# Forming block products for pairs of groups in a four-layer graph kernel

## The chip, the cores and the metric

The kernel runs on one NeuronCore of a Trainium2 chip. The metric is device time in microseconds of one execution, and lower is better. TensorE (PE in the profile) multiplies matrices into PSUM; VectorE (DVE), ScalarE (ACT) and GpSimd (POOL) do elementwise work; SyncE (SP) issues the DMAs. PSUM is used as eight banks of 512 fp32 values on each of 128 partitions. Everything is fp32.

## The reference

The input is a batch of 128 graphs of 64 nodes with 512 features, and a dense 64x64 adjacency for each graph. Four layers follow each other. Each adds its output to its input and then applies a layer norm over the features.

```python
# layer 0: graph attention with additive scores
y = x @ w;  s = y @ a
A = tanh((s_i + s_j) / 8) * 8;  A = leaky(A);  A = exp(A) * adj
A = A / sum(A) * sum(adj);      out = A @ x @ w
# layer 1: attention with adjacency as a factor
weight = adj * exp(q @ k.T);    out = (weight / sum(weight)) @ v
# layer 2: agg = adj @ (k * mask);  w = scale * mask * sum(q * agg)
out = softmax(w) * v
# layer 3: two hypergraph convolutions, 512 -> 1024 -> 512
h = layer_norm(relu(D H B H.T (x @ W1.T) + b1))
out = D H B H.T (h @ W2.T) + b2 + x
# after each layer
x = layer_norm(x + out)
```

The kernel rewrites these. In layers 1 and 2, q @ k.T becomes x @ (Wq.T Wk) @ x.T, so that one 512x512 matrix (m1, m2) is made once and stands for two. The graph operators, which are 64x64, are applied ahead of the dense products.

## The kernel before

**Tiling.** The 8192 rows (128 graphs of 64 nodes) form 64 tiles of 128 rows. Two tiles are a *group* (`GT = 2`, 256 tokens), so there are `NG = 32` groups. Two groups are a *pair* (`SG = 2`), and two groups share a chunk of adjacency (`GC = 2`).

**Seven products for eight.** A dense product of a group is cut into 2x2 blocks, and done with seven block products in place of eight, by sums of the left blocks (`side_sums`, L915) and sums of the weights' blocks (t1 to t4, made once by `combine`, L527). `seven_products` (L953) calls `products_of` (L957), whose inner `times` (L967) emits the matmuls of one block product. It holds two banks, which go on accumulating from product to product: after each one its bank is evicted by `first` (the first write to a block of the result) or `more` (an addition to it), and only then may the next product add to that bank. A third bank takes the one product that stands apart.

**Row blocks before.** In a single group the two row blocks are its two tiles, 128 tokens each. A block product has 128 tokens, 256 features in depth (512 for 3b) and 256 output columns, so half a bank is filled. For w0, v1, v2 and 3b a block of tokens is the stationary operand and 256 columns of weights move past it (`width = D // 2`, L963). For m1 and m2 (`across=True`) the result is wanted transposed: blocks of weights are stationary, and the 128 tokens move:

```python
for c in range(2):
    for k in range(chunks):
        nc.tensor.matmul(o[:, ts(c, P)], b[:, k, ts(c, P)], l[:, k, :], ...)
```

Evictions go through `scaled_into` (L1019, w0, v2, 3b: one scaled add on DVE of 128x256), `plain_into` (L1032, v1) and `z_into` (L1199, m1, m2: ACT writes, DVE adds).

**Steps of a group.** `run(g)` (L1226) goes from step 0 to 12: scores of layer 0 (0), gathering x by the graph (1, `gathered` L893), w0 and layer norm (2), transposes (3), m1 and v1 (4), scores (5), attention and layer norm (6), transposes (7), m2 (8), scores (9), softmax (10), v2 and layer norm (11), gathering for layer 3 (12). Each step works on one group. After two groups, `run_rest(n)` (L1354) does layer 3 for both: 3a by two levels of the seven-product scheme, 49 small products with the two groups as row blocks (`pair_left_side` L941, `forty_nine_products` L1104), then bias, relu and layer norm of each h (13), gathering (14) and 3b (15). 3b loads each weight piece once for the pair but multiplies each group apart. The pairs in `APART_3A`, which hold groups 0, 1, 30 and 31, do layer 3 with groups alone.

**Weights.** m1 and m2 stay in SBUF (`RESIDENT`). The pieces of w0, v1, v2, 3a and 3b lie in DRAM and are loaded by `streamed` (L748) into the tiles called ring when a product needs them; w0, v1 and v2 are three loads of 512 KB and one of 256 KB for each group.

**Order.** Operations are not emitted in the order of the code. `order.add` records each with its engine, an estimated cost and a key (`BASE[g]` + step - `EARLY[step]`). `Order.run` then plans all five engines: it goes forward in planned time and starts on each free engine the ready operation with the lowest key, if there are free tiles for it. The kinds of tiles and their number (L334 to L344: x 6, k4 17, ring 9, bank 8, ...) set how much may be under way, and at most three products at once are (`kinds["product"]`, L345). The plan also knows the array's division: most matmuls use all 128x128 of it, gathers use 64x64 quarters, scores use 64-column halves, and a change between them has a planned price. `pinned` (L1473) then fixes the order of each engine. All traced lines are therefore that helper's, L1479, and operations are told apart by tiles and shapes. `PREPARED` and `LEAD` shift the preparation of weights and the halves of a pair's layer 3.

Of the kernel before, what the change touches and what calls it, by code (L numbers as in the profile page):

```python
# [13 lines left out]
ALU = mybir.AluOpType  # L14
# [17 lines left out]
    3.2735, 8.0652, 5.7526, 12.3539, 15.2711, 19.4819, 28.2783, 26.7823,  # L32
    36.0674, 38.5696, 41.9228, 44.5673, 49.736, 57.2555, 62.3073, 66.8928,
    72.8672, 74.4107, 83.6469, 85.3215, 91.7972, 98.2815, 105.3829, 104.8263,
    113.3204, 117.0908, 123.649, 125.591, 132.4907, 135.1692, 144.8875, 142.169,
# [3 lines left out]
LEAD = [18.6707, 10.0037]  # L39
PREPARED = [3.2501, 6.4884, 8.4096, 18.9837, 15.9208, -1.3348]  # L40
# [29 lines left out]
class Order:  # L70
    LATENCY = {"PE": 210, "DVE": 125, "ACT": 140, "POOL": 120, "SP": 3500}
    AGAIN = {"PE": 0, "DVE": 115, "ACT": 115, "POOL": 120}
    TO_PE = 0
    BYTES_PER_NS = 270
    UNDERWAY = 9
    TURN, TURN_DIVIDED = 110, 60

    NEAR = 0.004
    FAR = 163.3543
    ENOUGH = 1.2457  # L80

    EARLY = [7.5201, -0.713, 2.7673, 21.1569, 0.5055, 0.6085, 5.6889, 14.9021, 0.0162, 18.6753, 16.5455, 0.4227, -1.4983, -1.1338, 12.9793, -2.8031]
# [3 lines left out]
    AHEAD = 5.2259  # L86
    TOGETHER = 0.3719
    OLDEST = 3.3813
    SPARE = {"k4": 1, "ring": 0}
# [35 lines left out]
    def keys_by_what_follows(self):  # L125
# [15 lines left out]
        for o in self.ops:  # L141
            if o.led and o.group is not None:
                gone = self.TOGETHER * (o.step - o.led.step)
                o.step, o.key = o.step - gone, o.key - gone

# [150 lines left out]
def kernel(  # L296
# [37 lines left out]
    kind("x", 6, GT, D)  # L334
    kind("k4", 17, PIECE)
    kind("ring", 9, PIECE)
# [430 lines left out]


# [457 lines left out]
    def run(g):  # L1226

        def step(k):
            order.key, order.early, order.group = BASE[g] + float(k), order.EARLY[k], g

        step(0)
        xt = xs.pop(g)
        adj, turned, gm, am, sums, g1, dc, dh = prepared[g // GC]
        own = slice(g % GC * GT, g % GC * GT + GT)
        at_x = block_views(xt, lambda: xt.t)
        of_x = lambda t: xt[[2 * t, 2 * t + 1]], lambda t, rows, at: xt.t[rows, t, at : at + N]


        s = Buf("col", GT)
        diag, e, ps_s = Buf("e", GT), Buf("e", GT), Buf("bank")  # L1240
        for t in range(GT):
            row_dot([xt[[2 * t, 2 * t + 1]], u0_b], s[t], lambda t=t: xt.t[:, t, :], lambda: u0_b.t)
            act(N + 40, [s[t]], [diag[t]], lambda t=t: nc.scalar.activation(diag.t[:, t], eye, AF.Identity, scale=s.t[:, t : t + 1]))

        over_graph(diag, ps_s)
        for t in range(GT):
            act(N + 40, [ps_s, s[t]], [e[t]], lambda t=t: nc.scalar.activation(
                e.t[:, t], tiles(ps_s)[:, t], AF.Tanh, bias=s.t[:, t : t + 1]), NOW)
        dve(GT * N, [e], [e], lambda: nc.vector.scalar_tensor_tensor(e.t, e.t, 0.1, e.t, ALU.mult, ALU.max))
        act(GT * N, [e], [e], lambda: nc.scalar.activation(e.t, e.t, AF.Exp, scale=8.0))  # L1250
        dve(GT * N, [e, adj], [e], lambda: nc.vector.tensor_mul(e.t, e.t, adj.t[:, own]))

        ps_e = Buf("bank")
        over_graph(e, ps_e)
        rs = Buf("e")
        dve(7 * GT * N, [ps_e], [rs], lambda: nc.vector.reciprocal(flat(rs.t), ps_e.t[:, : GT * N]), NOW)
        dve(GT * N, [e, rs], [e], lambda: nc.vector.tensor_mul(e.t, e.t, rs.t))
        step(1)
        left = left_side(gathered(*of_x, lambda h, t: e.t[halves[h][0], t, :], [e]))
        step(2)  # L1260
        sx = Buf("col", 2 * GT)
        seven_products(*left, first_use["w0"] if g == 0 else streamed("w0"), *scaled_into(
            at_x, sums, slice(2 * CT + own.start, 2 * CT + own.stop), D // 2, sx))
        layer_norm(xt, sx)


        step(3)
        xT = transposed(xt, turn=True)

        for t in range(GT):  # L1270
            pool(D, [xt[[2 * t, 2 * t + 1]], bv_b], [xt[[2 * t, 2 * t + 1]]],
                 lambda t=t: nc.gpsimd.tensor_add(xt.t[:, t, :], xt.t[:, t, :], bv_b.t))
        left = left_side(xT)
        step(4)
        zT = Buf("k4", 4)
        seven_products(*left, first_use["m1"] if g == 0 or "m1" in RESIDENT else streamed("m1"), *z_into(zT, u1_c), across=True)
        v = Buf("k4", 4)
        seven_products(*left, first_use["v1"] if g == 0 else streamed("v1"), *plain_into(v))
        step(5)
        ps_w = scores(xT, zT)  # L1280
        e1 = Buf("e")
        act(GT * N, [ps_w], [e1], lambda: nc.scalar.activation(e1.t, tiles(ps_w), AF.Exp), NOW)
        dve(GT * N, [e1, turned], [e1], lambda: nc.vector.tensor_mul(e1.t, e1.t, turned.t[:, own]))
        step(6)
        f = Buf("col")
        ps_f = Buf("bank")
        pe(110, [e1], [ps_f], lambda: nc.tensor.matmul(ps_f.t[:, :GT], flat(e1.t), row_of, start=True, stop=True))
        dve(GT, [ps_f], [f], lambda: nc.vector.reciprocal(f.t[:, :GT], ps_f.t[:, :GT]), NOW)
        po = [Buf("bank") for _ in range(GT)]
        sx = Buf("col", GT)  # L1290

        def emit_po():

            for h, (cols, _) in enumerate(halves):
                for t, (rows, _) in enumerate(halves):
                    nc.tensor.matmul(po[t].t[cols], e1.t[rows, h, :], v.t[rows, ts(h, D)], start=True, stop=True)

        pe(w_pe(D), [e1, v], po, emit_po, mode="quarters", matmuls=4)
        for t in range(GT):
            dve(D + 110, [po[t], f, xt[[2 * t, 2 * t + 1]]], [xt[[2 * t, 2 * t + 1]], sx[t]],  # L1300
                lambda t=t, sx=sx: nc.vector.scalar_tensor_tensor(
                    xt.t[:, t, :], po[t].t, f.t[:, t : t + 1], xt.t[:, t, :], ALU.mult, ALU.add, accum_out=sx.t[:, t : t + 1]), NOW)
        layer_norm(xt, sx, 1)

        step(7)
        xT2 = transposed(xt)
        left = left_side(xT2)
        step(8)
        zT2 = Buf("k4", 4)
        seven_products(*left, m2 if "m2" in RESIDENT else streamed("m2"), *z_into(zT2), across=True)  # L1310
        step(9)
        ps_w2 = scores(xT2, zT2)
        pr = Buf("e")
        dve(GT * N, [ps_w2, am], [pr], lambda: nc.vector.tensor_mul(pr.t, tiles(ps_w2), am.t[:, own]), NOW)
        step(10)

        ps_p = Buf("bank")
        over_graph(pr, ps_p)
        mx, sw, wc = Buf("col"), Buf("col"), Buf("col")
        dve(GT * N, [ps_p], [mx], lambda: nc.vector.tensor_reduce(mx.t[:, :GT], tiles(ps_p), AX.X, ALU.max), NOW)  # L1320
        dve(GT, [mx], [mx], lambda: nc.vector.tensor_scalar(mx.t[:, :GT], mx.t[:, :GT], -SCALE, None, ALU.mult), NOW)
        e2 = Buf("e", GT)
# [227 lines left out]
```

## Time and profile before

| | |
|---|---|
| median of 3 runs | 2146.41 us (2145.26 to 2149.38) |
| the profiled execution | 2145.31 us, of which the span 2143.4 us |
| instructions in the trace | 53774, of which 21433 matmul passes |
| TensorE clock granted | 0.998 of full speed |
| busy: PE 99%, weight loads 85%, DVE 66%, ACT 56%, POOL 21% | of the span |
| DMA | 418.92 MB on the main queue, 56.8% of 16 engines' span |
| loads of w0, v1, v2 | 93 + 189 of 512 KB, 31 + 63 of 256 KB |
| k,m passes (m1, m2) | 3584 of 128x128 |
| ring,k passes of 256 columns | 4828; ring,h (3b) 1024 |

A matmul row has a start and a length, but the lengths of neighbours overlap, so the time from one start to the next tells what a matmul costs in a run of its kind. PEld is the load of the stationary operand. An fp32 matmul of the code stands as two rows (passes) in the trace, a transpose as one. Names like `bank<-ring,k` say what is written and read: weights in ring against tokens in k4; `k,m` is m1 or m2, and `ring,h` is 3b or the sums that 3b lays into h.

### The profile page before, as it was taken

The numbers are of one execution on the slowest core, as the hardware profiler recorded it, in microseconds if no ns is written. First come the engines' busy times: TensorE is split into PE (matmuls) and PEld (weight loads), VectorE is DVE, ScalarE is ACT, GpSimd is POOL, SyncE is SP. The second block draws the span as 40 slices with busy tenths as digits, with TensorE's granted clock in tenths as the row PEclk, the third lists the DMA queues.
The fourth block names the chain that finished last, engine by engine and source line by source line (L and its number), as shares of the span: only waits on it lengthen the run. The fifth ranks groups of instructions, "written<-read, shape, count | busy, mean of one in ns | idle before, by whom it ended". The sixth has DMA issues, their size and how long they took to land.

```text
span 2143.4 us, 53774 instructions
## 1 busy us (share of the span) xinstructions
PE 2123.4 (99%) x21433; PEld 1829.4 (85%) x21433; DVE 1407.9 (66%) x4150; ACT 1197.9 (56%) x2698; POOL 458.0 (21%) x434
## 2 busy tenths in 40 slices
PE   8999999999999999999999999999999999999997
PEld 4887788888889888888888888888888988888875
DVE  5766667675864767667586766766777576676744
ACT  3545566473655565656455655646656456564635
POOL 1211142212211221220212202122130222203111
PEclk9999999999999999999999999999999999999999
DMA  9778866645644647456455646554554554645555
GB/s 295 229 269 303 281 226 250 208 165 183 227 163 147 205 153 244 144 191 211 156 179 183 213 145 207 181 190 165 185 200 154 199 194 152 214 164 172 179 180 179
DMA packets 166315, 422.35 MB, mean 197 GB/s; under 512 B 34929, under 2 KB 52529, under 8 KB 166065
## 3 DMA queue, kind: packets, MB, share of 16 engines
q1 hardware_dynamic: 166064, 418.92, 56.8%
q8 instruction: 169, 2.77, 0.5%
q14 instruction: 82, 0.66, 0.1%
HBM read 382.77 MB, written 36.08 MB: 195 GB/s over the span
## 4 chain that ended last, share of the span: by engine, by line
PE 99%; ACT 0%; DMA 0%; DVE 0%; issue 0%; SPq 0%; POOLq 0%; ACTq 0%; DVEq 0%
PE bank L1479 99%; DMA k<-in_wk_dram 0%; ACT k L1479 0%; SPq L1479 0%; DVE e L1479 0%; ACT h L1479 0%; ACT x L1479 0%; DVE h L1479 0%; DVE col L1479 0%; POOLq L1546 0%; ACTq L1546 0%; DVE m L1479 0%; ACT e L1479 0%; DVE x L1479 0%; ACT kept L1479 0%
## 5 line engine op out<-in xcount | busy, mean ns | idle before, releaser
L1479 PE MATMUL bank<-ring,k 128*128 128x256 f32 (+1 forms) x4940 | 1187.8, 387 | 1.3 <-ACT k L1479 1.3
L1479 PEld LDWEIGHTS bank<-ring,k 128*128 128x128 f32 x4940 | 898.2, 190 | 150.2 <-issue 28.4
L1479 ACT COPY k<-bank 128x256 f32<-128x256 f32 (+1 forms) x934 | 429.3, 485 | 402.5 <-PE bank L1479 386.3
L1479 DVE SCALAR_TENSOR_TENSOR x<-bank,col,x 128x256 f32<-128x256 f32 (+1 forms) x736 | 363.3, 504 | 281.3 <-PE bank L1479 275.2
L1479 PEld LDWEIGHTS bank<-k,m 128*128 128x128 f32 x3584 | 436.2, 192 | 19.1 <-issue 4.0
L1479 PE MATMUL bank<-k,m 128*128 128x128 f32 x3584 | 448.5, 276 | 0.0
L1479 DVE TENSOR_TENSOR k<-bank,k 128x256 f32<-128x256 f32 x582 | 236.0, 420 | 181.9 <-PE bank L1479 118.4
L1479 POOL TENSOR_TENSOR col<-col,mhalf 128x2 f32<-128x2 f32 (+1 forms) x161 | 111.9, 695 | 1139.1 <-DVE col L1479 860.8
L1479 ACT ACTIVATE k<-x,col 128x512 f32<-128x512 f32 x256 | 184.3, 722 | 253.4 <-DVE col L1479 241.7
L1479 ACT ACTIVATE x<-x,col,col 128x512 f32<-128x512 f32 x256 | 199.5, 815 | 63.3 <-DVE col L1479 63.0
L1479 PE MATMUL bank<-ring,h 128*128 128x256 f32 x1024 | 233.3, 380 | 0.0
L1479 PEld LDWEIGHTS bank<-ring,h 128*128 128x128 f32 x1024 | 192.3, 190 | 26.9 <-ACT k L1479 0.8
L1479 DVE TENSOR_TENSOR k<-k,k 128x256 f32<-128x256 f32 (+2 forms) x361 | 179.1, 505 | 0.4
L1479 DVE TENSOR_TENSOR k<-k 128x256 f32<-128x256 f32 (+2 forms) x349 | 152.9, 457 | 37.0 <-ACT k L1479 33.8
L1479 ACT ACTIVATE k<-bank,u_c 128x128 f32<-128x128 f32 x256 | 85.8, 371 | 65.7 <-PE bank L1479 60.9
L1479 PE MATMUL bank<-k,k 128*64 128x64 f32 (+1 forms) x2112 | 111.7, 239 | 4.7 <-DMA k<-in_wk_dram 4.6
L1479 POOL TENSOR_TENSOR k<-k,b3b_b 128x512 f32<-128x512 f32 x64 | 81.2, 1272 | 150.7 <-DVE k L1479 93.0
L1479 PEld LDWEIGHTS bank<-k,k 128*64 128x64 f32 (+1 forms) x2112 | 79.7, 140 | 37.3 <-issue 18.1
L1479 POOL TENSOR_TENSOR x<-x,bv_b 128x512 f32<-128x512 f32 x64 | 81.4, 1280 | 115.1 <-PE bank L1479 38.9
L1479 DVE TENSOR_SCALAR col<-col 128x2 f32<-128x2 f32 (+2 forms) x402 | 71.5, 185 | 41.2 <-ACT k L1479 34.7
L1479 DVE TENSOR_TENSOR h<-k,k 128x1024 f32<-128x1024 f32 (+1 forms) x88 | 91.0, 1041 | 7.7 <-ACT k L1479 7.2
L1479 POOL TENSOR_TENSOR x<-x,k 128x512 f32<-128x512 f32 x64 | 81.4, 1273 | 40.8 <-DVE k L1479 28.4
(102 smaller groups left out, 1627.3 us busy)
## 6 DMA issues: line engine op xcount, KB each, us to landing
ring<-3a SPq DMA_DIRECT2D x196, 512.0 KB, 4.3
ring<-v SPq DMA_DIRECT2D x189, 512.0 KB, 4.2
ring<-3b SPq DMA_DIRECT2D x126, 512.0 KB, 4.3
ring<-w SPq DMA_DIRECT2D x93, 512.0 KB, 4.4
x<-in_x_dram SPq DMA_DIRECT2D x32, 512.0 KB, 5.2
ring<-v SPq DMA_DIRECT2D x63, 256.0 KB, 4.1
out_dram<-x SPq DMA_DIRECT2D x31, 512.0 KB, 4.5
ring<-w SPq DMA_DIRECT2D x31, 256.0 KB, 4.4
```

The source lines that it names most:

```text
L1479: made = f(*args, **kwargs)
```

## The change

`run` now takes a list of groups and does all steps, 0 to 15, for them together; `run_rest` and its waiting list are gone. The groups of `APART_3A` are still run one by one, through the old functions. For the other 14 pairs each dense product is made once per pair: the two groups are the two row blocks (256 tokens each), so a block product has 256 tokens and 256 output columns and fills a bank of 512. The weights of w0, v1 and v2 are streamed once for a pair, as those of 3b were. For m1 and m2 256 tokens move past each weight block. A block product is recorded as two PE operations, one for each half of the bank.

```diff
-    kind("x", 6, GT, D)
+    kind("x", 7, GT, D)
     kind("k4", 17, PIECE)
-    kind("ring", 9, PIECE)
+    kind("ring", 8, PIECE)
...
+    def pair_products(a, s, pieces, first, more, across=False, chunks=KC // 2):
+        going, pair = Buf("product"), [Buf("bank") for _ in range(2)]
+        pieces = iter(pieces)
+        def times(token, left, start=True):
+            piece, view = next(pieces)
+            def emit(u):
+                l, b, o = left[1](), view(), token.t
+                for k in range(chunks):
+                    w, v = (b[:, k, ts(u, P)], l[:, k, :]) if across else (l[:, k, ts(u, P)], b[:, k, :])
+                    nc.tensor.matmul(o[:, ts(u, D // 2)], w, v, start=start and k == 0 and u == 0,
+                                     stop=k == chunks - 1, skip_group_check=True)
+            for u in range(2):
+                pe(w_pe(D // 2, chunks), [left[0], piece, going], [token], lambda u=u: emit(u), matmuls=chunks)
+            return (token, going), lambda: token.t
+        first("11", *times(pair[0], a["11"]))
+        first("22", *times(pair[1], s[0]))
+        more("11", *times(Buf("bank"), a["12"]))
+        first("12", *times(pair[0], s[1], False))
+        more("12", *times(pair[1], s[3], False))
+        more("22", *times(pair[0], s[2], False))
+        first("21", *times(pair[0], a["22"], False))
+
+    def pair_scaled_into(xs_, fs, sums):
+        def add(k, token, ps, last):
+            xt, (f, at), r, j = xs_[row(k)], fs[row(k)], row(k), col(k)
+            for t in range(GT):
+                cell, c = xt[2 * t + j], 2 * t + j
+                dve(D // 2 + 40 + 70 * last, [*token, f, cell], [cell, *([sums[r][c]] if last else [])],
+                    lambda t=t, c=c: nc.vector.scalar_tensor_tensor(
+                        xt.t[:, t, ts(j, D // 2)], ps()[:, ts(t, D // 2)], f.t[:, at + t : at + t + 1], xt.t[:, t, ts(j, D // 2)],
+                        ALU.mult, ALU.add, **({"accum_out": sums[r].t[:, c : c + 1]} if last else {})), NOW)
...
+    def pair_z_into(zs, bias=None):
...
+        def first(k, token, ps):
+            if bias is None:
+                act(D, [*token], [at(k)[0]], lambda: nc.scalar.copy(at(k)[1](), two(ps)), NOW)
...
+        def more(k, token, ps):
+            dve(D, [*token, at(k)[0]], [at(k)[0]], lambda: nc.vector.tensor_add(at(k)[1](), two(ps), at(k)[1]()), NOW)
...
-    def run(g):
+    def run(groups):
+        n, last_of = len(groups), groups[-1]
...
+        def left_of(xT):
+            return pair_left_side(xT) if n == SG else left_side(xT[0])
...
+        left = left_of(xT)
         step(4)
+        zT = [Buf("k4", 4) for _ in groups]
...
+        if n == SG:
+            pair_products(*left, m1_pieces, *pair_z_into(zT, u1_c), across=True)
+        else:
+            seven_products(*left, m1_pieces, *z_into(zT[0], u1_c), across=True)
+        vs = [Buf("k4", 4) for _ in groups]
+        if n == SG:
+            pair_products(*left, of_pair("v1", last_of), *pair_plain_into(vs))
...
-        products_of(sides, streamed("3b"))
...
+            pair_products(a, s_, streamed("3b"), *pair_scaled_into([xt_[g] for g in groups], scales, [sx[g] for g in groups]), chunks=KH // 2)
...
-        run(g)
-        if len(waiting) == SG or g // SG in APART_3A:
-            run_rest(len(waiting))
+        if g // SG in APART_3A:
+            run([g])
+        elif g % SG == SG - 1:
+            run(list(range(g - SG + 1, g + 1)))
```

Two smaller edits come with it. In layer 2's softmax the row sum of e2 is made by ACT with the exponential (`accum_out`), where DVE made it with a reduction. And the constants of the plan have new values:

```diff
-    3.2735, 8.0652, 5.7526, 12.3539, 15.2711, 19.4819, 28.2783, 26.7823,
+    6.0035, 8.2772, 13.2033, 17.6332, 26.0202, 27.1146, 41.4888, 43.61,
...
-LEAD = [18.6707, 10.0037]
-PREPARED = [3.2501, 6.4884, 8.4096, 18.9837, 15.9208, -1.3348]
+LEAD = [37.2697, 5.5754]
+PREPARED = [28.6382, 16.68, 12.9121, 14.55, 17.8769, 0.587]
...
-    TO_PE = 0
-    BYTES_PER_NS = 270
-    UNDERWAY = 9
+    TO_PE = 50
+    BYTES_PER_NS = 260
+    UNDERWAY = 8
...
-    NEAR = 0.004
-    FAR = 163.3543
-    ENOUGH = 1.2457
+    NEAR = 27.7595
+    FAR = 251.4563
+    ENOUGH = 0.0205
...
-    AHEAD = 5.2259
-    TOGETHER = 0.3719
-    OLDEST = 3.3813
-    SPARE = {"k4": 1, "ring": 0}
+    AHEAD = 15.591
+    TOGETHER = 0.0013
+    OLDEST = 1000000000.0
+    SPARE = {"k4": 0, "ring": 1}
```

The step constants `EARLY` and the rest of `BASE` change likewise. `NEAR`, `FAR` and `ENOUGH` govern when the planner turns from the whole array to a divided one, `UNDERWAY` how many loads may be in flight, and `SPARE` how many free tiles operations far ahead of the oldest must leave.

## The prediction

> **What bounds the kernel now.** I began with the page's busy shares and its chain of the work that ended last.
>
> ```profile
> PE 2123.4 (99%) x21433; PEld 1829.4 (85%) x21433; DVE 1407.9 (66%) x4150; ACT 1197.9 (56%) x2698; POOL 458.0 (21%) x434
> ...
> PE 99%; ACT 0%; DMA 0%; DVE 0%; issue 0%; SPq 0%; POOLq 0%; ACTq 0%; DVEq 0%
> ```
>
> TensorE's matmuls (PE) cover 99% of the span, and the chain never leaves them. But is that engine full, or only never empty? The Trainium skill ("Perfetto Trace Analysis", section "Identifying the Most-Contended Engine") warns that matmul busy time is a poor measure, because matmuls overlap, and asks for the busy share of weight loads. By that rule 85% leaves 15%, some 314 us, in which PE would wait; looser waits would then be worth more than fewer columns. So I looked at start times, which overlap cannot flatter: the timeline of PE's matmuls (start, length, engine, line, operation, tiles, shape, count).
>
> ```profile
> 643.37 3.62 PE L1479 MATMUL bank<-ring,h 128*128 128x256 f32 x16
> 646.82 3.62 PE L1479 MATMUL bank<-ring,k 128*128 128x256 f32 x16
> 650.27 3.73 PE L1479 MATMUL bank<-k,m 128*128 128x128 f32 x32
> 653.85 1.03 PE L1479 MATMUL bank<-ring,k 128*128 128x256 f32 x4
> ...
> 704.77 1.03 PE L1479 MATMUL bank<-ring,k 128*128 128x256 f32 x4
> 705.73 1.15 PE L1479 MATMUL bank<-k,k 128*64 128x64 f32 x32
> 706.81 1.99 PE L1479 MATMUL bank<-ring,k 128*128 128x256 f32 x8
> ```
>
> Sixteen 256-column passes take 646.82 - 643.37 = 3.45 us, 0.216 each; 32 passes of 128 columns take 653.85 - 650.27 = 3.58 us, 0.112 each. (The page has two such records, or passes, for each fp32 matmul in the code.) Such pitches hold throughout: I priced every pass of the program at the start-to-start time of its shape, and every change of the array's division at 0.10 us, and the sum is about 2090 us of a span of 2143. The rest is 4 us before the first matmul, some 10 in the start-up, 9.5 after the last matmul, and small pauses of 0.02 to 0.1 us spread evenly. So the row decides against the rule's reading: PE is full. The waits confirm it: these are all of PE's.
>
> ```profile
> PE bank L1479 <- DMA k<-in_wk_dram: 4.6, 2, 4.3
> PE bank L1479 <- DVE e L1479: 2.9, 2, 1.6
> PE bank L1479 <- ACT k L1479: 1.3, 1, 1.3
> PE bank L1479 <- issue: 0.6, 1, 0.6
> PE bank L1479 <- ACT x L1479: 0.4, 1, 0.4
> PE bank L1479 <- ACT m L1479: 0.3, 1, 0.3
> PE bank L1479 <- ACT kept L1479: 0.2, 1, 0.2
> ```
>
> Ten microseconds in all (columns: total, times, longest), nearly all at the very start. What shortens PE's list shortens the kernel; what relieves DVE, ACT, POOL or DMA does not, as long as no new wait appears.
>
> **The change, part by part.** Groups 0, 1, 30 and 31 still run alone; the other 28 become 14 pairs.
>
> *m1 and m2.* Each product of a single group issues 28 matmuls of 128 columns; a pair issues 28 of 256 for both groups. For 28 groups, two products and two passes, 3136 passes at 0.112 us (351.2 us) become 1568 at 0.216 (338.7): **-12.5 us**. A rule promises far more. The Trainium skill ("TensorE: Matmul & The Clock Gate", section "Back-to-back issue gap") gives, for a stream in which every matmul has its own weight load, about 81 ns at 128 columns and 131 at 512. A straight line gives 98 at 256 (my estimate from that page), so merging two saves 64 of 162, 40%, here 139 us. The trace says that weight loads are hidden already, for 0.112 is within 4% of half of 0.216. I take the row. The exact form, 256 columns of k against weights out of m, is not in the trace; the nearest row, ring,h, also has a new weight load for each pass and runs at 0.216. The ends are -12.5 and, should these run only as fast as now, 0.
>
> *w0, v1, v2, 3b.* Each piece of weights is 256 columns that move past 128 tokens, before and after; two token blocks of two groups become four blocks in one product. Passes and columns are the same: 0 us. The order of PE's instructions agrees: 2414 + 512 matmuls of 256 columns against ring tiles in both programs, 784 new ones against m, 224 of 128 columns left over for the four single groups.
>
> *Switches of the array.* Scores and gathers divide the array; each change costs PE. In the rows above the four passes before 705.73 need 0.86, so the divided ones begin 0.10 late, and these 32, which follow each other at 30 ns on average, hand back 0.11 late. The new planned order has 370 changes where the old one has 427, since longer products mean fewer seams and the constants of the plan are new: 57 x 0.10 = **-5.7 us**. The ends are 0 and -7.
>
> *Small pauses.* The trace has about 170 of 0.10 us between 256-column passes with no wait behind them, about one to 64 matmuls. With 783 fewer matmuls of 10973, some 12 go: **-1 us**.
>
> *Evictions.* These are what could hurt.
>
> ```profile
> L1479 DVE SCALAR_TENSOR_TENSOR x<-bank,col,x 128x256 f32<-128x256 f32 x672 | 318.1, 481 | 265.1 <-PE bank L1479 259.2 <-ACT k L1479 0.4
> L1479 ACT COPY k<-bank 128x512 f32<-128x512 f32 x482 | 269.3, 588 | 156.2 <-PE bank L1479 152.4 <-ACT h L1479 0.8 <-DVE k L1479 0.5
> L1479 DVE TENSOR_TENSOR k<-bank,k 128x256 f32<-128x256 f32 x582 | 236.0, 420 | 181.9 <-PE bank L1479 118.4 <-ACT k L1479 57.3 <-ACT kept L1479 0.3
> ```
>
> A full bank takes ACT 0.59 us instead of about 0.37, DVE about 0.69 (its 512-wide add out of a bank, h<-bank,h, mean 687 ns) instead of 0.42, and for w0, v2 and 3b two instructions of 0.48. PE may go on with that bank only afterwards. In the old order a waiting matmul often has just 0.86 us of other matmuls since the last one that the awaited engine needed, and PE does not stall, so the hand-overs both ways cost at most 0.86 - 0.48 = 0.38. The new need is then 0.97 for ACT, 1.07 for DVE and 1.34 for the two scaled adds. In the new order, of the 112 places where a pair's m1 or m2 goes on in a bank that must first be emptied, the shortest cover is 1.09 us and all but two have 1.3; for the sites behind a 256-wide scaled add 95% have 1.55 or more; for 3b the least is 1.73. Over all of PE's waits, those with under 0.8 us of such cover fall from 18 to 6. I cost the evictions at 0; if every one of the 84 pair products (14 pairs, six stages) lost 0.1 us, at +8.
>
> *Busy totals elsewhere.* DVE drops 126 adds out of banks net (about -19 us), turns 336 side sums of 256 into 168 of 512 (336 x 0.465 - 168 x 0.70, -39 us) and loses 32 reductions of e2 (-9), whose sums ACT now makes with 64 accumulator reads (64 x 0.19 = +12, inside ACT's idle 44%). All of it lies beside PE: 0 us.
>
> *DMA.* w0, v1 and v2 come once per pair: 42 streams fewer, each three loads of 512 KB and one of 256, together 77 of 419 MB. The queues were 57% busy and PE waited for no load after the start: 0. One ring tile fewer (8 for 9) takes cover away, but the shortest distance in matmul time from a freed ring to its first user is 5.8 us against 6.1, and a load lands in 4.3. SP also issues 168 fewer loads.
>
> *Start and tail.* The first 40 us in the new order have two matmuls directly behind an engine that needs the matmul before, where the old one has four, worth 1.7, 1.4, 0.5 and 0.3 us: **-1 us**, ends -3 and +2. The last 40 us have the same sequence of one group's 3a and 3b.
>
> **Sum:** -12.5 - 5.7 - 1 - 1 = -20.2 us, plus 1 for single short waits I cannot place: -19. The profiled execution took 2145.3 us (2 of them outside its span), which gives 2126; the median of the runs shown is 1.1 above it, so 2126 to 2127. I say 2126.
>
> **The rivals.**
> - *As summed*, 2120 to 2132: 0.73.
> - *Part is handed back* through evictions twice as long, at 0.1 to 0.2 us per pair product: 84 x 0.13 = 11 us, 2137. For it: full banks, and two scaled adds in a row. Against: the covers above. 0.12.
> - *Lockstep starves PE*, the case on the other side. Two groups now finish w0 together and both need their layer norm (two scaled adds 0.96, four small DVE steps 0.75, two squares 1.44, POOL's power 0.70, a scale of 0.82: 4.7 us and hand-overs) before m1 can begin, where before the other group's products filled in. With 14 pairs and four such places there are 56 stops. It takes 24.7/56 = 0.44 us each to be slower than before by 0.2%; at 1 us each the time is 2182. For it: 17 k4 tiles now hold pairs. The skill's "Consistent bubbles" (same page, "Identifying Performance Opportunities") says that a repeated gap can mean too few buffers. Against: seven x tiles, so a third pair is under way, and the covers listed. 0.12, of which 0.05 ends within 0.2%.
> - *Weight loads were worth more than the pitch shows*: towards the rule's -139 us, anything under 2118. 0.03.
>
> That the change doesn't do what it says is excluded by the order of instructions.
>
> **How the numbers follow.** A measurement of this kernel tells 0.2% (4.3 us) from no change. Faster: 0.73 + 0.12 + 0.03 = 0.88; same 0.05; slower 0.07. The range takes in the first case and most of the second: 2118 to 2140.
>
> **What would show it.** Right: k,m rows of 128x256 at a pitch of 0.216; PE still 99%; waits of PE within 10 us; some 77 MB less moved; busy times of DVE and ACT some 70 and 35 us lower. Wrong: waits of PE on ACT k, DVE x or DVE k that repeat in each pair, or gaps of PE at the layer norms.

## The result and the profile after

| | before | after |
|---|---|---|
| median | 2146.99 us (2145.26 to 2149.38, 4 runs) | 2114.22 us (2114.03 to 2114.51, 4 runs) |
| the profiled execution, its span | 2145.3, 2143.4 us | 2114.4, 2112.6 us |
| PE's passes | 21433 | 19867 |
| changes of the array's division, in the program | 427 | 370 |

The ratio is 0.9847, 95% interval 0.983 to 0.9864: 32.8 us faster by the medians, 30.8 by the spans of the two profiled executions. The prediction said 2126, with 2118 as the lower end, so the direction was right and the gain was more than half as large again as its sum.

The page of after, the lines that answer to those of before (busy shares; the chain that ended last; the DMA queue that moves data: packets, MB, share):

```profile
PE 2097.3 (99%) x19867; PEld 1773.1 (84%) x19867; DVE 1361.7 (64%) x3768; ACT 1168.2 (55%) x2538; POOL 458.3 (22%) x434
...
q1 hardware_dynamic: 141872, 341.83, 47.4%
...
PE 98%; ACT 1%; DMA 0%; DVE 0%; issue 0%; SPq 0%; POOL 0%; POOLq 0%; ACTq 0%; DVEq 0%
```

All of PE's waits in after (us in total, times, longest):

```profile
PE bank L1602 <- DMA k<-in_wk_dram: 5.5, 2, 4.2
PE bank L1602 <- DVE e L1602: 1.6, 2, 1.1
PE bank L1602 <- ACT k L1602: 1.0, 2, 0.7
PE bank L1602 <- ACT e L1602: 0.4, 1, 0.4
PE bank L1602 <- ACT x L1602: 0.2, 1, 0.2
```

The same engine bounds the kernel as before, with 8.7 us of waits. The loads fell from 418.92 to 341.83 MB, DVE's busy time by 46 us, ACT's by 30, and none of that shows in the chain. Seven groups of waits became five. The only one behind a layer norm's last step (ACT x, a gather that waits for its x) is 0.2 us. The new form of m1 and m2 can be read off PE's timeline (start, length, operation, shape, count):

```profile
584.30 7.07 PE L1602 MATMUL bank<-k,m 128*128 128x256 f32 x32
591.21 1.03 PE L1602 MATMUL bank<-ring,k 128*128 128x256 f32 x4
```

Thirty-two passes take 591.21 - 584.30 = 6.91 us, 0.216 each, the pitch taken from the ring rows of before.

**Where the time came from.** I gave every pass of both traces the time to the start of the next pass, took off the pitch of its shape, and sorted the rest by where it lies:

| part of PE's span (us) | before | after | difference | predicted |
|---|---|---|---|---|
| passes of m1, m2 at their pitch | 401.5 | 389.0 | -12.5 | -12.5 |
| other passes of the whole array at their pitch | 1420.0 | 1419.8 | -0.2 | 0 |
| edges of divided stretches: in, out, and from one divided form to the other (0.09 to 0.11 each) | 43.0 | 37.2 | -5.7 | -5.7 |
| divided passes, stalls among them included | 233.6 | 227.0 | -6.7 | part of "start" |
| pauses in the whole array after the first 60 us | 26.5 | 22.2 | -4.3 | -1 |
| the first 60 us, first matmul and jitter | 8.9 | 10.4 | +1.5 | -1 |
| start of the last matmul to the end of the span | 9.8 | 7.1 | -2.8 | 0 |
| sum | 2143.4 | 2112.6 | -30.8 | -20.2, +1 for unplaced waits |

The two large terms came out to a tenth of a microsecond. Both rows are counts times a pitch or an edge read in the traces, so this says that the counts and those prices were right, not that they were the whole price. Three small rows did not come out: the pauses, the divided passes and the tail.

Two things in these traces lie across the rows. Of the 57 changes that went, 36 are between the whole array and a divided one (184 divided stretches became 166) and 21 between the two divided forms, 64x64 quarters and 64-column halves (61 became 40). And the clock was not the same throughout. Two stretches of before (busy time and count of PE, PEld, DVE, ACT and POOL; then the granted clock of PE, the DMA share and GB/s):

```profile
20.00:24.60 4.60, 2.65 (x33) 1.05 (x34) 4.00 (x10) 2.54 (x12) 1.26 (x1) 1.00 0.97 359
24.70:28.10 3.40, 3.40 (x49) 2.09 (x40) 3.40 (x9) 1.42 (x3) 0.00 (x0) 0.50 0.91 234
```

For 3.4 us of its start-up before was granted half the clock, which can have cost it 1.7 us at most; after has no such stretch. This part of the gain is in the rows of the first 60 us and of the divided passes.

### The profile page after: what moved, and what is told of

Its sections match the earlier page's. It is cut to its first block, busy times and chain, and to the rows that moved or that the text cites. A ratio compares the mean times of both kernels' runs of the same rounds, so it can differ in the third digit from the quotient of the medians.

```text
span 2112.6 us, 49594 instructions
## 1 busy us (share of the span) xinstructions
PE 2097.3 (99%) x19867; PEld 1773.1 (84%) x19867; DVE 1361.7 (64%) x3768; ACT 1168.2 (55%) x2538; POOL 458.3 (22%) x434
## 3 DMA queue, kind: packets, MB, share of 16 engines
q1 hardware_dynamic: 141872, 341.83, 47.4%
## 4 chain that ended last, share of the span: by engine, by line
PE 98%; ACT 1%; DMA 0%; DVE 0%; issue 0%; SPq 0%; POOL 0%; POOLq 0%; ACTq 0%; DVEq 0%
PE bank L1602 98%; ACT k L1602 1%; DMA k<-in_wk_dram 0%; DVE e L1602 0%; ACT x L1602 0%; SPq L1602 0%; ACT e L1602 0%; ACT m L1602 0%; DVE col L1602 0%; DVE k L1602 0%; POOL col L1602 0%; DVE m L1602 0%; POOLq L1669 0%; DVE x L1602 0%; ACT bw_b L1602 0%
## 5 line engine op out<-in xcount | busy, mean ns | idle before, releaser
L1602 PEld LDWEIGHTS bank<-ring,k 128*128 128x128 f32 x4940 | 916.8, 190 | 146.8 <-issue 24.5
L1602 ACT COPY k<-bank 128x512 f32<-128x512 f32 (+1 forms) x822 | 406.7, 529 | 368.0 <-PE bank L1602 365.0
L1602 DVE SCALAR_TENSOR_TENSOR x<-bank,col,x 128x256 f32<-128x256 f32 (+1 forms) x736 | 341.3, 503 | 218.6 <-PE bank L1602 204.8
L1602 PE MATMUL bank<-k,m 128*128 128x256 f32 (+1 forms) x2016 | 426.7, 358 | 0.7 <-ACT k L1602 0.7
L1602 PEld LDWEIGHTS bank<-k,m 128*128 128x128 f32 x2016 | 347.4, 190 | 43.9 <-issue 1.9
L1602 DVE TENSOR_TENSOR k<-bank,k 128x256 f32<-128x256 f32 (+1 forms) x456 | 216.2, 494 | 158.4 <-PE bank L1602 107.4
L1602 DVE TENSOR_TENSOR k<-k,k 128x512 f32<-128x512 f32 (+3 forms) x319 | 191.6, 617 | 4.0 <-ACT k L1602 3.7
L1602 DVE TENSOR_TENSOR k<-k 128x256 f32<-128x256 f32 (+2 forms) x223 | 113.9, 526 | 61.7 <-ACT k L1602 53.5
L1602 POOL TENSOR_TENSOR k<-k,k 128x1024 f32<-128x1024 f32 (+1 forms) x31 | 72.1, 2326 | 182.0 <-DVE h L1602 65.9
L1602 ACT ACTIVATE k<-bank,u_c 128x256 f32<-128x256 f32 (+1 forms) x144 | 59.9, 445 | 65.2 <-PE bank L1602 65.1
```

The source lines that it names most:

```text
L1602: made = f(*args, **kwargs)
```

## Experiments

Eleven kernels ran. The kernel before, timed beside each batch, had medians of 2145.07, 2146.2 and 2144.88 us.

| kernel | median us (lowest to highest) | ratio to before, 95% |
|---|---|---|
| narrow_m | 2124.93 (2124.61 to 2127.41) | 0.9908, 0.9891 to 0.9924 |
| old_traffic | 2118.66 (2117.54 to 2119.16) | 0.9874, 0.986 to 0.9889 |
| before_split_tail | 2143.18 (2141.79 to 2145.76) | 0.9991, 0.9984 to 0.9998 |
| pairs_old_plan | 2231.03 (2230.21 to 2234.94) | 1.0402, 1.0387 to 1.0418 |
| more_switches | 2129.72 (2127.66 to 2129.79) | 0.9921, 0.9907 to 0.9934 |
| old_early | 2311.52 (2310.55 to 2314.24) | 1.0773, 1.0758 to 1.0788 |
| double_evict | 2138.98 (2138.56 to 2139.57) | 0.9967, 0.9955 to 0.9979 |
| no_single | 2138.45 (2137.52 to 2142.16) | 0.9967, 0.9954 to 0.9979 |
| forced_switches | 2250.95 (2250.59 to 2251.67) | 1.0495, 1.0478 to 1.0513 |
| forced_whole | 2169.83 (2169.59 to 2170.59) | 1.0117, 1.0102 to 1.0132 |
| long_blocks | 2118.69 (2117.36 to 2119.78) | 0.9877, 0.9863 to 0.9892 |

### narrow_m: is it the wider pass, and do pauses go with the number of matmuls?

The kernel after, with each matmul of a pair's m1 and m2 cut into two of 128 columns, in the same plan.

```diff
-                for k in range(chunks):
-                    w, v = (b[:, k, ts(u, P)], l[:, k, :]) if across else ...
+                for c in range(2 if across else 1):
+                    n = D // 4 if across else D // 2
+                    for k in range(chunks):
+                        w, v = (b[:, k, ts(u, P)], l[:, k, ts(c, n)]) if across else ...
```

> The changed kernel with the pairs' m1 and m2 issued as two matmuls of 128 columns each in place of one of 256; plan and order as in the changed kernel. Column theory: 1568 passes of 256 columns become 3136 of 128, so 1568 x (2 x 0.112 - 0.216) = +12.5 us, 2127. Theory that the small pauses go with the number of matmuls: besides, pauses of PE rise from 22 towards 26.5 us (the 784 matmuls are back), +4 to +5, 2131. Theory that they go with traffic or with the plan: pauses stay near 22, 2127.

Its row of m1 and m2 has the old form and count again:

```profile
L1605 PE MATMUL bank<-k,m 128*128 128x128 f32 x3584 | 438.0, 276 | 0.7 <-ACT k L1605 0.7
```

The time at pitch rises by 12.55 us (389.0 to 401.5) and the span by 10.4, to 2123.0. So the 256-column form is worth about what the pitch said. But 784 more matmuls bring no more pauses: after 60 us there are 21.5 us of them where after has 22.2. The step "one pause to 64 matmuls" is refuted.

### old_traffic: were the loads worth anything?

The kernel after, which after each piece of w0, v1 or v2 also copies that piece from DRAM to a DRAM buffer that nothing reads.

```diff
+            nc.sync.dma_start(out=idle[turns[0] % 8][:, : n * width], in_=src.t[:, : n * width])
```

> The changed kernel with a second, unused transfer of each piece of w0, v1 and v2 from DRAM to DRAM right behind the real one (208 transfers, some 95 MB); the output is unchanged and the PE order too. Theory that the pauses go with DMA traffic: pauses back at 26 us or more, 2118 to 2121. Theories of matmul count and of plan: pauses near 22, 2114 to 2115.

The queue moves 95 MB more and is busier than in before; the lines of its page and of PE's waits that changed most:

```profile
q1 hardware_dynamic: 154352, 437.27, 58.3%
```

```profile
PE bank L1610 <- ACT e L1610: 1.8, 3, 1.0
...
PE bank L1610 <- DVE x L1610: 1.1, 2, 0.8
...
PE bank L1610 <- ACT x L1610: 0.8, 1, 0.8
```

The span grows by 4.3 us, as six or so short waits on other engines; the pauses inside matmuls stay (19.9 us against 19.4). These 95 MB do not slow PE's passes. The kernel adds 208 issues and another kind of transfer, so its 4.3 us is only a rough mark for what the 77 MB saved can have been worth; the account of after leaves little room for it.

### before_split_tail: the tail

The kernel before splits the last layer norm by tiles only for `g == NG - 1`, which is group 31. This kernel does it for groups 30 and 31.

```diff
-            for among in (range(t, t + 1) for t in range(GT)) if g == NG - 1 else (range(GT),):
+            for among in (range(t, t + 1) for t in range(GT)) if g >= NG - 2 else (range(GT),):
```

> The kernel before, with the final layer norm of groups 30 and 31 both by single tiles (before: 31 alone). If the shorter tail of the changed kernel comes only from which of the two groups ends last: last matmul start to end of span falls from 9.8 to 7.1 us, the time by 2.8 us, 2144. If it comes from something else, the tail stays near 9.8 and the time at 2147.

The ends of the two timelines tell why. In before, both tiles go together (128x2, two tiles in one row of ACT):

```profile
2136.80 0.70 POOL L1479 TENSOR_TENSOR col<-col,mhalf 128x2 f32<-128x2 f32 x1 [10.30 <-DVE col L1479]
2137.53 0.16 DVE L1479 TENSOR_TENSOR col<-col,col 128x2 f32<-128x2 f32 x1 [0.88 <-POOL col L1479]
2137.72 1.52 ACT L1479 ACTIVATE x<-x,col,col 128x512 f32<-128x512 f32 x2 [1.27 <-DVE col L1479]
```

In after, the first tile is finished while the second still waits for POOL:

```profile
2107.67 0.80 ACT L1602 ACTIVATE x<-x,col,col 128x512 f32<-128x512 f32 x1
2107.80 0.15 DVE L1602 TENSOR_SCALAR col<-col 128x1 f32<-128x1 f32 x1 [0.24 <-ACT k L1602]
2108.09 0.56 POOL L1602 TENSOR_TENSOR col<-col,mhalf 128x1 f32<-128x1 f32 x1 [0.73 <-DVE col L1602]
```

So in before the planned order let group 30 end last, unsplit; in after it is group 31. Splitting both in before shortens the part behind the last matmul from 9.84 to 7.04 us, to after's 7.06. The median falls by only 1.9 us, with an interval that just excludes no change. The span of the profiled execution is 0.8 us shorter: 2.0 of the 2.8 us come back elsewhere in that trace (1.2 in the divided stretches, 0.7 in the first 60 us), and why was not looked into.

### pairs_old_plan and old_early: is lockstep a danger at all?

The code of after, with all constants of its plan set back to before's (pairs_old_plan), or only `EARLY` and `LEAD` (old_early).

```diff
-LEAD = [37.2697, 5.5754]
+LEAD = [18.6707, 10.0037]
...
-    EARLY = [14.4537, -21.4408, 7.6077, 25.6747, ...]
+    EARLY = [7.5201, -0.713, 2.7673, 21.1569, ...]
```

> The pair structure with all the plan's constants of the kernel before (BASE, EARLY, LEAD, PREPARED, SPARE and the others). Its PE order has 388 changes of the array's division (changed kernel 370, before 427). If the new constants only set the number of changes and the group that ends last: +1.8 us and +2.8 us, 2119. If they are what keeps PE free of waits in lockstep: waits of PE go from 9 us to 20 or more, 2125 to 2145.

> The kernel after, with two sets of constants of its plan set back to those of the kernel before: how much earlier or later each step of a group is due, and the lead of the steps. The order has 393 changes of division (+23) and 112 waits of PE with under 0.8 us of cover where the kernel after has 6, the old plan on the pairs 69. If such waits are what costs (the old plan lost 84 us in waits and in slower divided stretches, about 1.2 us for each): 2114 + 3 + 106 x 1.2 = 2240, with PE's waits on DVE x, ACT x and DVE e of many us. If the old plan lost its time for another reason (its due times of the groups, its margins), waits stay under 20 us and the time is 2117 to 2130.

The first waits of PE in pairs_old_plan, and in old_early:

```profile
PE bank L1602 <- DVE k L1602: 19.0, 15, 5.1
PE bank L1602 <- ACT x L1602: 17.4, 11, 3.8
PE bank L1602 <- ACT k L1602: 12.8, 14, 1.8
```

```profile
PE bank L1602 <- DVE e L1602: 29.1, 9, 6.4
PE bank L1602 <- ACT x L1602: 27.7, 16, 3.5
PE bank L1602 <- DVE k L1602: 26.4, 24, 3.8
```

With the old constants the same pair code is slower than before, by 4.0% and 7.7%. The waits on ACT x stand ahead of gathers and transposes of an x that a layer norm has just finished, as the rival on the other side said; the other waits are hand-overs elsewhere. The constants that the change brings with it keep them off, and among those `EARLY` and `LEAD` decide. Old values of those two among otherwise new ones do worse than a wholly old set: they are a set, not single improvements.

The count of waits with little cover ranks the kernels rightly (6 under 0.8 us in after, 69 in pairs_old_plan, 112 in old_early). 1.2 us for each was expected in old_early, and (2311.5 - 2114.2 - 3) / 106 = 1.8 was paid. PE's waits explain only part of this: they rise from 8.7 to 136.5 us, which is 1.2 for each. Much of the rest goes with the clock. old_early has 19 stretches at half the granted clock, 119.5 us of its span, and pairs_old_plan ten, 78.5 us; a pass of 256 columns has a pitch of 0.427 us there for 0.216. The passes of the whole array alone are 37 and 32 us longer in them, and half of each total, 60 and 39 us, is the most that they can have cost. So here a wait cost its length and more, though no run changed the clock by itself.

### double_evict: how near are the evictions?

ScalarE copies each of the 112 first banks of v1 and m2 of the pairs twice.

```diff
-  act(D, [*token], [at(k)[0]], lambda: nc.scalar.copy(at(k)[1](), two(ps)), NOW)
+  act(D, [*token], [at(k)[0]], lambda: [nc.scalar.copy(at(k)[1](), two(ps)) for _ in range(2)], NOW)
```

The v1 eviction is changed in the same way.

> The kernel after, with ScalarE copying each of the 112 first banks of the pairs' v1 and m2 products twice (once more 0.59 us each, 66 us of ScalarE in all), in the same order on TensorE. If covers decide, as the prediction costed evictions: a full bank needs about 0.97 us and has 1.09 or more now, so it costs nothing now; with 1.56 needed some 60 of these hand-overs are short by 0.2 to 0.5 us, so 2114 + 8 to 20, and PE's waits on ACT k grow from 1.0 us to about 10. If evictions lie far from PE's path: 2114 to 2116, no new waits. If they already cost something today: more than 30 us.

```profile
PE bank L1602 <- ACT k L1602: 10.3, 26, 1.0
```

The waits on ACT k come to the 10 us that the covers gave, in 26 places where the covers gave some 60. The kernel as a whole loses 24.8 us, more than expected: 16.4 in waits ahead of matmuls, 4.8 in divided stretches, 3.2 in pauses inside matmuls. So the step "evictions at 0" holds (in after PE waits 1.0 us on ACT k), but without much in hand: some 26 of the 112 places have no further 0.59 us to give.

### no_single: the four single groups in pairs too

```diff
-APART_3A = (0, NG // SG - 1)
+APART_3A = ()
```

> The kernel after, with groups 0, 1, 30 and 31 in pairs too, so that all 32 groups run as 16 pairs. 448 more passes of 128 columns become 224 of 256 (-1.8 us), and PE's list, priced pass by pass and change by change, is 2063.7 us instead of 2071.3, -7.6, with 18 waits under 0.8 us of cover instead of 6, all at the two ends. If PE's list sets the time: 2107. If the first pair starves at the start (both layer norms before anything else is there) and the last pair has a longer tail (both groups' last layer norm after the last product, some +2 to +5 us) the gain is given back: 2112 to 2122.

```profile
PE bank L1602 <- ACT h L1602: 9.5, 1, 9.5
PE bank L1602 <- ACT e L1602: 5.6, 2, 5.2
```

PE's passes at their pitch are 8.0 us shorter, and the kernel is 24 us slower than after. One wait of 9.5 us stands at 2083, where the last pair's layer 3 has no other pair beside it; the tail is 2.6 us longer, and all of PE's waits together are 29.7 us where after has 8.7. In and behind three of them (5.2, 9.5 and 2.4 us long) PE has half the clock, for 30.7 us in all. The longest of them, and a row of PE in it:

```profile
2084.40:2101.50 17.10, 6.66 (x135) 5.96 (x136) 6.50 (x11) 14.02 (x22) 1.39 (x2) 0.50 0.15 57
```

```profile
2093.37 3.69 PE L1602 MATMUL bank<-kept,h 64*64 64x64 f32 x128 [9.49 <-ACT h L1602]
```

A row of 128 such passes took 2.05 us at the full clock in long_blocks, below. Single groups at the ends are worth their narrow passes. I had expected at most 8 us of loss: the cost of an end without other work was mis-sized there, by the waits and by the half clock that goes with them.

### more_switches: the plan with more changes of division

The kernel after with three constants of the plan set back, which leaves the work alone and gives 417 changes for 370.

```diff
-    TO_PE = 50
-    BYTES_PER_NS = 260
-    UNDERWAY = 8
+    TO_PE = 0
+    BYTES_PER_NS = 270
+    UNDERWAY = 9
```

> The kernel after, with three constants of its plan (the delay of a hand-over to TensorE, the load rate and the number of loads under way) set back to those of the kernel before. The work is the same; the planned order has 417 changes of the array's division instead of 370, and 12 instead of 6 waits of PE with under 0.8 us of cover. Theory A (a divided stretch costs 0.20 us, 0.10 in and 0.10 out, and the pauses inside matmuls go with the number of matmuls, which differs by 7 of 10190): 2114.2 + 47 x 0.10 = 2119, pauses inside matmuls stay at about 208. Theory B (a return to the whole array also leaves a pause of about 0.10 us inside one of the first four matmuls, so that a stretch costs some 0.33): 24 more stretches, 2114.2 + 24 x 0.33 = 2122, and 20 to 30 pauses inside matmuls more.

It is 15.5 us slower than after, twice what theory B gave and three times theory A. Pauses directly behind a return to the whole array rise from 146 to 165, with 17 returns more, which fits B and not A. But other pauses and short waits in the whole array grow by 6.2 us, and 3.4 us at half clock (at 68 us) are new, so this kernel doesn't isolate the price of a change. The next pair does.

### forced_switches and forced_whole: the price of a change by itself

At 252 places, ahead of each fresh bank of a pair product, two small matmuls are added in a divided array; the control adds one matmul with the whole array at the same places. The product that follows overwrites the bank.

```diff
+                if start and u == 0:
+                    for rows, _ in halves:
+                        nc.tensor.matmul(o[rows, :P], same[rows, rows], ident[rows, :], start=True, stop=True)
```

```diff
+                if start and u == 0:
+                    nc.tensor.matmul(o[:, :P], same, ident, start=True, stop=True)
```

> The kernel after, with two small matmuls that divide the array (64 x 64 weights, 128 columns) ahead of each of the three fresh banks of every pair product, into the bank that the product then overwrites: 252 sites, 504 matmuls, 482 more changes of division (852 instead of 370), the plan otherwise the same. The small matmuls themselves, at the 15 ns of a pass in the row of divided ones, are 504 x 0.030 = 15 us. If a change costs 0.10 us, as the prediction took it: + 48, together 2114 + 63 = 2178. If it costs the 0.24 to 0.30 us that the comparison of before, after and more_switches gives, changes and all that hangs on them: + 116 to 145, together 2245 to 2274. If only the parts seen in each stretch count (0.093 in, 0.05 in the first round, 0.11 out, 0.04 as a pause of 0.10 after 4 in 10): 241 x 0.30 = 72, together 2201. Pauses inside matmuls: 208 plus some 100 if they belong to returns from a divided array, plus 8 if they go with the number of matmuls.

> The control to forced_switches: at the same 252 sites one small matmul of 128 columns with the whole array (504 passes), with no change of division more than after. At the pitch of such passes, 0.109 to 0.112 us: 504 x 0.11 = 55, together 2169 to 2171, with about 208 pauses inside matmuls, PE's waits within 12 us as before. If added matmuls cost more than their pitch (a pause for each 64 matmuls, or an upset plan), 2175 or more.

The control came out at 2169.83, right at the pitch (504 x 0.11 = 55), with 199 pauses inside matmuls for 208. Added matmuls alone cost nothing beyond their passes. The divided ones cost 136.7 us. How much of it the changes cost depends on what the added passes cost by themselves. With the expectation's 0.015 a pass it would be 122 / 482 = 0.25 us a change, but that is the pace of 64-column passes on all four quarters, and these have 128 columns on two. In after, ten runs of four such passes inside a longer divided stretch begin with steps of 0.020 and 0.092, 0.11 for two, 0.056 a pass; this leaves (136.7 - 1008 x 0.056) / 482 = **0.17 us a change**. With 0.044, the mean of all such passes in after, it is 0.19. One such place in PE's timeline of forced_switches, and then the same place in the control:

```profile
73.30 1.03 PE L1605 MATMUL bank<-ring,k 128*128 128x256 f32 x4
74.26 0.43 PE L1605 MATMUL bank<-ident,same 64*64 64x128 f32 x4
74.63 1.13 PE L1605 MATMUL bank<-ring,k 128*128 128x256 f32 x4
75.59 0.38 PE L1605 MATMUL bank<-e,same 128*128 128x128 f32 x2
```

```profile
73.59 1.03 PE L1604 MATMUL bank<-ring,k 128*128 128x256 f32 x4
74.45 0.39 PE L1604 MATMUL bank<-ident,same 128*128 128x128 f32 x2
74.67 1.03 PE L1604 MATMUL bank<-ring,k 128*128 128x256 f32 x4
75.54 0.27 PE L1604 MATMUL bank<-e,same 128*128 128x128 f32 x1
```

In the control, each block of four passes takes 0.86 or 0.87 us and the matmul between them 0.22. In forced_switches the block ahead takes 0.96 (0.10 to go in), the divided four 0.37, and the block *behind* takes 75.59 - 74.63 = 0.96 as well. The place costs 0.57 us in all, of which 0.22 are its four passes: 0.35 for going and coming back. That last 0.10 is the point: it falls after the first pass that follows the return, between the two passes of one matmul, in every one of the 238 such places found in the trace (0.320 to the second pass, where 0.216 is the pitch). Pauses at that place of a return went from 146 to 384; in the control they stay at 146.

The kernel after has the same mark. Eight passes behind a divided stretch, and eight that no stretch touches:

```profile
704.32 1.63 PE L1602 MATMUL bank<-kept,h 64*64 64x64 f32 x96
705.88 1.99 PE L1602 MATMUL bank<-ring,k 128*128 128x256 f32 x8
707.80 0.69 PE L1602 MATMUL bank<-k,k 128*64 128x64 f32 x16
...
732.45 1.89 PE L1602 MATMUL bank<-ring,h 128*128 128x256 f32 x8
734.18 1.04 PE L1602 MATMUL bank<-ident,x 128*128 128x128 f32 x8
```

The first take 707.80 - 705.88 = 1.92 us, the second 734.18 - 732.45 = 1.73 = 8 x 0.216. Of the 0.19 between them, 0.10 is the way into the next divided stretch and 0.10 the pause after the last.

### long_blocks: fewer changes still?

The plan lets no more than 64 divided matmuls begin in 4.5 us. Here it is 128 in 9 us.

```diff
-    BLOCK = 64
-    REST = 4500
+    BLOCK = 128
+    REST = 9000
```

> The kernel after, with one rule of its plan widened: where no more than 64 divided matmuls may begin in 4.5 us, now 128 in 9 us. The work is the same; the planned order has 334 changes of division instead of 370 and 9 instead of 6 waits of PE under 0.8 us of cover. If a change costs 0.10 us: PE's list is 5.5 us shorter, 2109. If it costs 0.24 to 0.30: 5.5 + 36 x 0.14 to 0.20 more, 2102 to 2104. If longer divided stretches lower the granted clock or starve the product stream, or the three short waits more cost 1 us each: 2112 to 2120.

```profile
PE bank L1602 <- issue: 7.9, 8, 2.1
```

```profile
600.90 2.05 PE L1602 MATMUL bank<-kept,h 64*64 64x64 f32 x128
602.76 0.41 PE L1602 MATMUL bank<-e,x 64*64 64x64 f32 x16
604.46 0.40 PE L1602 MATMUL bank<-e,x 64*64 64x64 f32 x13 [1.29 <-issue]
```

With 36 changes fewer it is 4.5 us slower than after. PE stops eight times, 7.9 us in all, with no wait behind it: "issue" means that it waited for no semaphore that the profile shows. Behind one of the stops, at 237.7, PE has half the clock for 3.4 us, which is up to 1.7 more. Without both it would be near 2109. The 2102 to 2104 of the expectation rest on a price of 0.24 to 0.30 for each of the 36. They are 15 stretches (166 to 151) and 6 changes between divided forms; at 0.35 and 0.15 us, the prices of the next section, this is 6.2 us, or 2108.

What PE lacked in these stops may be read from the DMA queue called "instruction". One of its packets is all that the queues moved around the stop above (598 to 606 us; packets, MB, share):

```profile
q8 instruction: 1, 0.02, 1.0%
```

It landed at 603.09, and PE went on at 604.46, 1.37 us later. All eight stops end 1.27 to 1.60 us after such a packet landed. Of the seven other "issue" waits of PE in these thirteen traces five do so too, as the one at 1012.31 in before; two in old_early do not. after has 157 such packets for 39734 matmul passes and weight loads, narrow_m 169 for 42870: 253 and 254 to a packet. So PE seems to have run out of instructions. No run varied how they are fetched; this is argued and not shown. No plan that I ran beats the kernel after.

## Why the prediction was right in direction and wrong in size

- **PE is full, so its list sets the time: right.** The rows won against the two rules that the prediction quotes. The estimate that it draws from the Trainium skill ("TensorE: Matmul & The Clock Gate", section "Back-to-back issue gap"), 40% for merging two narrow passes, would have given 139 us; the merge gave 12.5 at the pitch, and taking it back cost 10.4 us of span (12.55 at the pitch). The measured time lies where the prediction put its rival "weight loads were worth more" (under 2118), but not by that cause.
- **w0, v1, v2, 3b at 0; DVE, ACT and DMA beside PE: right** within the account. DVE fell by 46 us instead of some 70, which changes nothing.
- **Evictions at 0: right**, with less in hand than "at +8 if every product lost 0.1" suggests.
- **Lockstep: right for this plan**, and the danger was real: two other plans on the same code and the same buffers fell to waits. (The section that the prediction cites on "Consistent bubbles" is in "Perfetto Trace Analysis" of the Trainium skill. Too few buffers, which it names as a possible cause, is not what separates these plans: with the same tiles the order alone made 2114 or 2312 us.)
- **Switches, "each change costs PE" 0.10 us: this is the step that failed, by size.** The rows that I read, 0.10 late going in and 0.11 late coming out, were right, and they gave the 5.7 us to the digit. They were not the whole price. The first round of divided passes behind any change, 0.107 us for 0.058, is 0.05 longer than later ones: 39 fewer of them, 1.9 us. And behind every return to the whole array the first pass holds 0.10 longer (0.05 where transposes follow), unless a 2-column product follows: 1.6 us (16.6 to 15.0). Together the changes gave 9.2 us for 5.7. A stretch costs 0.35 us (0.09 + 0.05 + 0.11 + 0.10) and a change between divided forms 0.15: 18 x 0.35 + 21 x 0.15 = 9.5. The evidence was in the trace of before, at the end of the very fence that the prediction shows. The next row there tells what the eight passes from 706.81 took, 1.83 us where 8 x 0.216 is 1.73:

```profile
706.81 1.99 PE L1479 MATMUL bank<-ring,k 128*128 128x256 f32 x8
708.64 0.38 PE L1479 MATMUL bank<-e,same 128*128 128x128 f32 x2
```

- **Small pauses, "about one to 64 matmuls": wrong cause.** Two equal rates, a pause to some 64 matmuls and a return to some 60, were taken for one law. Of the 169 pauses of about 0.10 us after the start-up of before, 154 stand directly behind the first pass after a return, as start times show, so the trace of before could have told the two apart. narrow_m added 784 matmuls and no pause, forced_switches added 238 returns and 238 pauses. Pauses in the whole array fell by 4.3 us instead of 1: the 1.6 above, and 2.7 of other small pauses and waits, which are not placed.
- **The divided stretches, 6.7 us that the sum did not have.** Some 4.0 are four single stalls that before had (1.33 and 0.50 at 50 us, 0.73 at 1011, 1.39 at 2090) and after has not. The first two belong to the prediction's "start: -1"; the other two were put at nothing. The last is the "ACT k 1.3" in the prediction's list of before's waits, which it took to lie nearly all at the start. 1.9 is the first rounds. Of the remainder, 0.8, some 0.5 is the divided run at 24.19 that before did at half clock. The first 60 us became 1.5 longer, though before's half clock lies there: other waits of the start-up grew.
- **Tail, "same sequence": wrong.** The sequence of PE is the same; that of the last group's layer norm is not, because another group is last. -2.8 us, put at nothing; of these before_split_tail shows 1.9 in the median.
- **+1 for waits that I could not place:** none came.

Put together: -12.7 for passes, -9.2 for changes of division, -2.7 for other pauses, -4.0 for stalls gone, -0.8 for the rest of the divided stretches, -2.8 for the tail, +1.5 for the start-up: -30.7 of 30.8. The medians give two more because the profiled execution of before lay 1.7 us under its median. No single term takes the sum out of its range. With changes of division at 9.2 us it would have been about 2123; it takes the tail, the stalls and the other pauses, all of them put at nothing or at 1 us, to come to 2114. That the new plan happened to remove the single stalls and to end on a split group was luck as far as the prediction goes: it had no step for them.

## What to carry to other kernels

Where one engine is full, price its list by start-to-start times, and price a change of state by an equal block of work *behind* it as well as by the edges: two blocks of eight passes, one after a change and one far from any, show in one subtraction what the edges hide. Before a rate is made a cause (a pause to so many matmuls), ask which other thing has the same count. Read the last ten microseconds of the two orders by group and tile, since little else runs there to hide what moves. And look at the granted clock stretch by stretch before a loss is put down to waits alone.

## What the runs showed of the hardware

- Changing from the whole array to a divided one and back costs PE 0.09 to 0.10 us in, about 0.05 in the first divided round, 0.11 out, and 0.10 behind the first pass after the return: some 0.35 us a stretch. In forced_switches a short stretch with four passes cost 0.57 us in all. A change between the two divided forms costs about 0.15.
- Whole-array passes hold 0.112 us at 128 columns and 0.216 at 256 while the queues move 95 MB more: the pauses inside matmuls were 19.9 us against 19.4.
- Plans that leave PE waiting show stretches at half the granted clock: none in after (8.7 us of waits), 3.4 us in before (10.3), 30.7 in no_single (29.7), 78.5 in pairs_old_plan (77.6), 119.5 in old_early (136.5). A pass of 256 columns has a pitch of 0.427 us in them.
- In long_blocks PE stopped eight times, for up to 2.1 us, with no wait that the profile shows. Ahead of the stops 126 to 211 passes had begun within 4.5 us, where in after 126 is the most in any 4.5 us and no such stop appears. The number alone does not decide it: from 806.2 us of long_blocks 225 passes began within 4.5 us and no stop followed. Each of the eight ended 1.27 to 1.60 us after a packet of the instruction queue had landed.
